# Layer 1 of six images by seven block products, and every set of seven products as seven tasks

## The chip, the core and the metric

The kernel runs on one core of a Trainium2 chip. The metric is device time in microseconds of one execution. The core has TensorE (PE, matrix products, with its weight loads listed apart as PEld), VectorE (DVE), ScalarE (ACT), GpSimd (POOL) and SyncE (SP), which mainly issues transfers (DMAs). Each engine works off its own instructions in order and waits on semaphores for the others. PE writes to PSUM[...]; everything else lies in SBUF.

## What is computed

Two layers run on x of shape (8, 32, 32, 256), all in float32. With N = 1024 tokens of C = 256 channels per image:

```
# layer 0, four heads of 256 channels
qkv   = xf @ W_qkv
atten = softmax over j of (q_i . k_j) / 16
res   = sum_j atten_ij v_j            # per head
x1    = concat(res) @ W_out + b_out + xf

# layer 1, 32 channels for f and g
f, g, h = x1 @ Wf + bf, x1 @ Wg + bg, x1 @ Wh + bh
b     = softmax over j of (g_i . f_j)
y     = gamma * (b @ h) + x1
```

The kernel folds the query and key weights of a head into one matrix, and the value and output weights into another, so that layer 0 needs only queries, scores, a product of the exponentials with x itself, and an output projection per head.

## The kernel before

**Units and steps.** A unit is one head of one image in layer 0 (`Layer0(b, h)`) or the whole layer 1 of one image (`Layer1(b)`). A unit has two blocks of 512 query tokens. A step is one block of one unit, and the list `steps` holds them in the order of the loop. Per image there are four layer-0 units, and layer 1 of the image before stands between head 1 and head 2 (`behind`), or behind head 3 for image 6 in the last round; layer 1 of image 7 is written out at the end.

**What a step issues.** The work is spread over three steps: step i issues the scores and half of the exponentials of its own block, the block sums, the key sums and most of the products of the block of step i-1, and the end of the products and the output projection of the block of step i-2. In the loop over `steps`, `put(tasks, *places)` gives each task a place, a number from about 0 to 10; at the end of the step the tasks are sorted by place and issued. PE, DVE and ACT keep exactly this order (`manual_schedule`); the planner orders POOL's and SP's instructions.

**Seven products.** `seven` (line 253 on, its matmuls on line 273) multiplies two matrices of 2 x 2 blocks with seven block products instead of eight, in three PSUM tiles z, y and x. `sum_a` and `sum_b` form the sums of blocks that it needs, four vector instructions each. It returns three tasks: `one` (products 1 and 6, copies e and u on ACT), `two` (products 5, 7 and 2, copy v, and the results 22 and 11), `three` (products 3 and 4, and the results 12 and 21). The results are vector additions of a PSUM tile and a copy (line 290). It serves the queries (`q`), the scores (`p`), the products of the exponentials with x (`y`) and the output projection (`o`).

**Layer 1 before.** `queries_apart` computes f and g (tile fg). `scores` makes 8 tiles of scores per block (`ps_l`, line 845) and their exponentials `s_l` (line 854). `values` computes h as rows for the image (`pr_v_l`, line 518, then line 828: times gamma, plus bias) with a column of ones behind it. `row_products` (line 933) multiplies the exponentials with these 257 columns, 8 matmuls for each of 4 tiles of tokens; the last column is the sum, and lines 941 and 943 divide and add x1.

**Sums and inverses of layer 0.** The block sums `ss` (line 638) are added up to `rs` (lines 645 and 649), `partition_all_reduce` on POOL (line 651) sums over the partitions into `rb`, two small transfers turn the row into columns (`line`, `st`), line 667 inverts, and two more spread the inverse over all partitions (`invb`). Line 725 scales the projection `o` by it, and a transfer issued on POOL (line 728) adds it to `x1T`. The sums `yt` of y (line 716) feed the output projection.

**Turning.** `squares` moves 32 x 32 squares by transfers, all issued on SP, and a vector transpose (line 418) turns each: from rows to columns for x (`turn_rows`), back for x1 (`turn_back`).

**Buffers.** The pools give the number of buffers per tag: `ps` 6 and `psm` 2 of the PSUM banks, `s` 2, `xT` 3, `v` 2, `m0` 1 (the tile o), `rs` 1, `rb` 1, `ss` 1.

Of the kernel before, what the change touches and what calls it, by code (L numbers as in the profile page):

```python
# [16 lines left out]
P = 128  # L17
# [3 lines left out]
def kernel(  # L21
# [67 lines left out]
    FAR = 2.0**64  # L89
# [163 lines left out]
    def seven(name, width, parts, matmuls, outs, tags, two_banks=False):  # L253
# [38 lines left out]
        def one():  # L292
            for k, number in (("z", 1), ("y", 6)):
                bank(k)
                product(k, number, k != "y" or not two_banks)
            nc.scalar.copy(scratch("e"), banks["z"])  # L296
            nc.scalar.copy(scratch("u"), banks["y"])

        def two():
            product("z", 5)  # L300
            product("y", 7)
            bank("x")
            product("x", 2, True)
            nc.scalar.copy(scratch("v"), banks["z"])  # L304
            add(outs["22"](), "y", sbs["v"])
            add(outs["11"](), "x", sbs["e"])

        def three():
            product("z", 3)
            product("y", 4)  # L310
            add(outs["12"](), "z", sbs["u"])
            add(outs["21"](), "y", sbs["e"])

        return [one, two, three]
# [64 lines left out]
    xT_of, x1T_of, xblocks, vblocks = {}, {}, {}, {}  # L379
# [16 lines left out]
    def squares(dst, src, swap):  # L396
# [5 lines left out]
        def move(a, c):  # L402
            for q in range(P // Q):
                to, rows_v = dst(), src()
                if swap:
                    nc.sync.dma_start(
                        to[ts(q, Q), :, c, ts(a, Q)], rows_v[ts(a, Q), c, :, ts(q, Q)]
                    )
                else:
                    nc.sync.dma_start(  # L410
                        to[ts(q, Q), c, :, ts(a, Q)], rows_v[ts(a, Q), :, c, ts(q, Q)]
                    )
# [48 lines left out]
    def value_sums(b):  # L461
# [3 lines left out]
        def piece(i):  # L465
            if i == 0:
                r = rows[b]
                t = tile_of("xt", [P, 4, NT // 2, P], f"xt_{b}")
# [3 lines left out]
                vblocks[b] = b_operands(blocks, sums)  # L472
# [61 lines left out]


    class Layer0:
# [82 lines left out]
        def sums(self, blk):  # L619
# [4 lines left out]
            made = {}  # L624

            def start():
                half = NT // 2
                p = self.p[blk]
                blocks = [p[:, ts(j, half), ts(e, HB)] for e in range(2) for j in range(2)]
                t = tile_of("ss", [P, 2, half, HB], f"ss_{n}")  # L630
                sums = [t[:, 1], t[:, 0], blocks[2], t[:, 0]]
                self.pblocks[blk] = a_operands(blocks, sums)
                made["t"], made["l"] = t, sum_a(sums, *blocks)

            def piece(i):
                if i == 0:
                    start()
                made["l"][i]()
# [8 lines left out]
            def last():  # L647
                r = made["r"]
                tt(r[:, 0, :], r[:, 0, :], r[:, 1, :], ALU.add)
                self.total[blk] = t = tile_of("rb", [P, NB], f"rb_{n}")  # L650
                nc.gpsimd.partition_all_reduce(  # L651
                    t, r.rearrange("p e i -> p (e i)"), P, bass_isa.ReduceOp.add
                )
                line = tile_of("line", [1, NB], f"line_{n}")
                nc.sync.dma_start(line, t[0:1, :])
                self.r[blk] = st = tile_of("st", [P, HT], f"st_{n}")
                with nc.allow_non_contiguous_dma(reason="a row of sums turns into columns"):
                    nc.sync.dma_start(st, line.rearrange("o (p t) -> p (o t)", p=P))

            adds = [partial(add, k) for k in range(1, NT // 2)]  # L660
            return [partial(piece, i) for i in range(4)], adds + [last]

        def invert(self, blk):
# [4 lines left out]
            if blk in self.rb:  # L668
                return
            line = tile_of("line", [1, NB], f"inv_{self.name}_{blk}")  # L670
            with nc.allow_non_contiguous_dma(reason="columns turn into a row"):
                nc.sync.dma_start(line.rearrange("o (p t) -> p (o t)", p=P), inv)
            self.rb[blk] = t = tile_of("invb", [P, NB], f"invb_{self.name}_{blk}")
            nc.sync.dma_start(t, line[0].partition_broadcast(P))
# [6 lines left out]
        def products(self, blk):  # L681


            def out(c, e):
                if blk not in self.y:
                    self.y[blk] = tile_of("y", [P, CC, NB], f"y_{self.name}_{blk}")
                return self.y[blk][:, c, ts(e, HB)].unsqueeze(1)

            return seven(
                f"y_{self.name}_{blk}", HB, 1,  # L690
                lambda number: [
                    (0, vblocks[self.b][number][:, j, :], self.pblocks[blk][number][:, j, :])
                    for j in range(NT // 2)
                ],
                {
                    "11": partial(out, 0, 0), "12": partial(out, 1, 0),
                    "21": partial(out, 0, 1), "22": partial(out, 1, 1),
                },
                NARROW,
            )  # L700

        def project(self, blk):
# [29 lines left out]
            return [partial(piece, i) for i in range(4)], seven(  # L732
# [7 lines left out]
            ), [add]  # L740


    class Layer1:
        scale = 1.0

        def __init__(self, b, direct=0):

            self.b, self.name, self.direct = b, f"{b}_l1", direct
            self.s = {}
            self.fg, self.v = None, None  # L750

# [23 lines left out]
        def queries_apart(self, tag=None):  # L775
# [7 lines left out]
            def task():  # L783
                fg = self.fg_tile()
                self.f, self.g = fg[:, 0, :], fg[:, 1, :]
                if tag is None:
# [33 lines left out]
        def values(self, last="psm"):  # L820
            def start():
                if self.v is None:
# [5 lines left out]
                lambda t2, pm: nc.vector.scalar_tensor_tensor(  # L828
                    self.v[:, 2 * t2 : 2 * t2 + 2, :C], pm, gamma_sb,
                    bh_sb.unsqueeze(1).broadcast_to([P, 2, C]), ALU.mult, ALU.add,  # L830
# [40 lines left out]
        def products(self, blk):  # L871
            return row_products(self, blk, rows1)

# [118 lines left out]
    steps, adds, exps = [], {}, {}  # L992

    for b in range(B):
        units = [Layer0(b, h) for h in range(HEADS)]
        if b > 0:
            units.insert(behind(b), Layer1(b - 1, NBLK))
        steps += [(u, blk) for u in units for blk in range(NBLK)]
# [9 lines left out]
    first_sums = value_sums(0)  # L1008
# [10 lines left out]
    for i, (a, blk) in enumerate(steps):  # L1019
        l0 = isinstance(a, Layer0)  # L1020
        one, two, nxt = step(i - 1), step(i - 2), step(i + 1)
        places = []

        def put(tasks, *at):
# [3 lines left out]
        if l0:  # L1028
            tasks, exps[i] = a.scores(blk)
            put(tasks, 0, 2, 4, 6, 8, 10)  # L1030
            put(exps[i][:2], 5.1, 6.1)
        else:
            tasks, _ = a.scores(blk)
            put(tasks, *((0.5, 2.4) if blk == 0 else (0.5, 2)))
        if is_l0(two):
            u, k = two
            put(u.products_of[k][2:], 1 if l0 else 0)
            if nxt is None:
                put([partial(u.invert_all, k)], 2.2)
            put([partial(u.invert, k)], 3.4 if l0 else 2.7)  # L1040
            ysums, tasks, adds[i] = u.project(k)
            put(ysums, *((1.1, 1.2, 1.3, 3.3) if l0 else (1.1, 1.2, 1.3, 2.5) if blk == 0 else
                         (0.6, 0.7, 0.8, 0.9)))
            put(tasks, *((3, 5.5, 7) if l0 else (4.5, 6, 7.2) if blk == 0 else
                         (3, 5, 7) if nxt else (1.9, 3.1, 4.1)))
            if nxt is None:
                put(adds[i], 4.2)
        if i - 1 in exps:
            put(exps[i - 1][2:], *((0.9, 0.91) if l0 else (0.1, 0.2)))
        if i - 1 in adds:  # L1050
            put(adds[i - 1], 0.5 if l0 or blk == 1 else 2.3)
        if is_l0(one):
            u, k = one
            sums, keys = u.sums(k)
            u.products_of[k] = u.products(k)
            put(sums, *((2.1, 3.2 if is_l0(two) else 2.4, 4.2, 5.6) if l0 else (0.8, 2.2, 3.5, 6.1)))
            put(keys, *((6.3, 6.6, 7.6, 8.7) if l0 else (6.3, 7.6, 8.3, 8.7)))
# [200 lines left out]
```

## Time and profile before

| | |
|---|---|
| median of 3 runs | 2305.96 us (2305.75 to 2306.03) |
| the profiled execution | 2305.9 us, of which its span is 2304.0 |
| PE busy | 2293.2 us, 10220 instructions |
| DVE busy | 1508.4 us, 2666 instructions |
| ACT busy | 756.9 us |
| POOL busy | 340.9 us |
| granted PE clock | 1.00 |
| layer-1 products, line 933 | 1024 PE instructions |
| layer-1 values, line 518 | 256 PE instructions |
| all-reduces, line 651 | 64, mean 3.226 us |
| transfers x1T<-o | 64, median 5.0 us from issue to landing |

Busy time is the time in which an engine has an instruction in work; the recorded durations of consecutive PE instructions overlap, so distances between starts are to be used for PE. A matmul in float32 appears as two PE records. In a line such as `psz<-q,xs 128x256 f32 x1024 | 264.6, 381` the names are the output and the inputs, then come shape and count, busy us and the mean ns of one. A bracket in the timeline tells how long the engine had been idle and what released it.

### The profile page before, as it was taken

How to read it: one execution, taken by the hardware profiler on the slowest of the kernel's cores; microseconds unless marked ns; L12 is line 12 of the kernel's file. 1: busy time of each engine (PE TensorE's matmuls, PEld its weight loads, DVE VectorE, ACT ScalarE, POOL GpSimd, SP SyncE). 2: the span in 40 equal slices, each digit the busy share in tenths (PEclk: the TensorE clock that was granted, in tenths of full speed). 3: DMA queues.
4: the chain of work that ended last, by engine and by line, in shares of the span. 5: the costliest groups of instructions: out<-in, count | busy, mean ns of one | idle time of the engine just before them, and what ended most of it. 6: DMA issues, size and time to landing. Idle time of an engine off the chain costs nothing.

```text
span 2304.0 us, 27262 instructions
## 1 busy us (share of the span) xinstructions
PE 2293.2 (100%) x10220; PEld 1887.2 (82%) x10220; DVE 1508.4 (65%) x2666; ACT 756.9 (33%) x1294; POOL 340.9 (15%) x243
## 2 busy tenths in 40 slices
PE   9999999999999999999999999999999999999999
PEld 7888888788887888788887888878888788888887
DVE  6776676476665766656766666656676557776663
ACT  3333333233332333323333233322333233333322
POOL 3111112011120112101121011210112101111211
PEclk9999999999999999999999999999999999999999
DMA  5111122301222113221132101321113211121222
GB/s 137 33 28 28 28 37 44 74 15 28 47 45 63 18 25 57 38 60 19 28 54 44 53 19 29 58 43 50 19 28 58 46 29 19 28 46 28 40 40 61
DMA packets 200925, 94.83 MB, mean 41 GB/s; under 512 B 165968, under 2 KB 170192, under 8 KB 200784
## 3 DMA queue, kind: packets, MB, share of 16 engines
q1 hardware_dynamic: 180176, 54.06, 11.2%
q0 software_dynamic: 20608, 38.94, 9.6%
q8 instruction: 83, 1.36, 0.2%
q14 instruction: 58, 0.48, 0.1%
HBM read 29.76 MB, written 8.65 MB: 17 GB/s over the span
## 4 chain that ended last, share of the span: by engine, by line
PE 98%; DVE 1%; DMA 1%; ACT 1%; issue 0%; ACTq 0%; SPq 0%
PE psz_y L273 14%; PE psy_y L273 14%; PE psz L273 14%; PE psy L273 14%; PE pa_l L933 10%; PE psz_o L273 7%; PE psx L273 5%; PE psx_y L273 5%; PE psz_q L273 3%; PE psy_q L273 3%; PE pr_v_l L518 3%; PE ps_l L845 1%; PE psx_q L273 1%; PE psx_o L273 1%; PE pm_fg L795 1%; DMA invb<-inv 0%
## 5 line engine op out<-in xcount | busy, mean ns | idle before, releaser
L651 POOL PARTITION_ALL_REDUCE rb<-rs x64 | 206.5, 3226 | 1448.8 <-issue 1153.4
L600 ACT ACTIVATE p<-p 128x1024 f32<-128x1024 f32 x256 | 263.9, 1056 | 74.5 <-DVE p L290 74.3
L273 PE MATMUL psz<-q,xs 128*128 128x256 f32 x1024 | 264.6, 381 | 0.0
L273 PE MATMUL psy<-qs,xs 128*128 128x256 f32 x1024 | 263.0, 379 | 1.2 <-DVE qs L579 1.2
L273 PE MATMUL psy_y<-p,xt 128*128 128x256 f32 x1024 | 241.9, 379 | 0.0
L933 PE MATMUL pa_l<-v_l,s_l 128*128 128x257 f32 x1024 | 232.1, 381 | 0.0
L273 PEld LDWEIGHTS psz<-q,xs 128*128 128x128 f32 x1024 | 192.9, 190 | 47.2 <-issue 19.1
L933 PEld LDWEIGHTS pa_l<-v_l,s_l 128*128 128x128 f32 x1024 | 193.7, 190 | 34.3 <-issue 6.8
L273 PEld LDWEIGHTS psy<-qs,xs 128*128 128x128 f32 x1024 | 193.3, 190 | 29.2 <-DVE qs L579 1.6
L296 ACT COPY e<-psz 128x512 f32<-128x512 f32 x128 | 75.1, 586 | 431.6 <-PE psz L273 431.6
L273 PEld LDWEIGHTS psy_y<-p,xt 128*128 128x128 f32 x1024 | 194.6, 190 | 26.4
L290 DVE TENSOR_TENSOR p<-psy,v 128x512 f32<-128x512 f32 x128 | 88.0, 688 | 87.7 <-ACT v L304 44.4
L728 POOL DMA_DIRECT2D x1T<-o x64 | 77.4, 1210 | 407.5 <-DVE o L725 354.2
L273 PE MATMUL psz<-q,x0T 128*128 128x256 f32 x512 | 131.4, 379 | 0.0
L273 PE MATMUL psx<-q,x0T 128*128 128x256 f32 x512 | 131.4, 379 | 0.0
L273 PE MATMUL psy<-qs,x0T 128*128 128x256 f32 x512 | 131.4, 379 | 0.0
L273 PE MATMUL psx_y<-p,x 128*128 128x256 f32 x512 | 121.0, 379 | 0.0
L273 PE MATMUL psz_y<-ss,x 128*128 128x256 f32 x512 | 121.0, 379 | 0.0
L273 PE MATMUL psy_y<-ss,xt 128*128 128x256 f32 x512 | 121.0, 379 | 0.0
L273 PE MATMUL psz_y<-p,x 128*128 128x256 f32 x512 | 120.9, 379 | 0.0
L273 PE MATMUL psz_y<-ss,xt 128*128 128x256 f32 x512 | 120.9, 379 | 0.0
L273 PEld LDWEIGHTS psz_y<-p,x 128*128 128x128 f32 x512 | 97.3, 190 | 20.9 <-PE psz_q L273 4.3
(153 smaller groups left out, 3700.5 us busy)
## 6 DMA issues: line engine op xcount, KB each, us to landing
x1T<-o POOLq DMA_DIRECT2D x64, 512.0 KB, 5.0
invb<-inv SPq DMA_DIRECT2D x63, 256.0 KB, 4.0
x<-x1T SPq DMA_DIRECT2D x256, 32.0 KB, 2.0
out_dram<-x SPq DMA_DIRECT2D x15, 512.0 KB
x<-in_x_dram SPq DMA_DIRECT2D x14, 512.0 KB, 4.4
x0T<-x SPq DMA_DIRECT2D x224, 32.0 KB, 2.0
fg<-v_l POOLq DMA_DIRECT2D x56, 64.0 KB, 2.0
w<-in_L_conv_W_qkv_dram POOLq DMA_DIRECT2D x36, 32.0 KB, 3.3
```

Source lines behind the costliest of these rows:

```text
L273: nc.tensor.matmul(banks[k][:, ts(i, w)], lhsT=lhsT, rhs=rhs, start=first and n == 0, stop=True, skip_group_check=True,)
L290: nc.vector.tensor_tensor(dst, shaped(banks[k]), shaped(other), ALU.add)
L296: nc.scalar.copy(scratch("e"), banks["z"])
L518: nc.tensor.matmul(pm[:, ts(j, C)], lhsT=src()[:, c, ts(2 * t2 + j, P)], rhs=w()[:, c, :], start=(c == 0), stop=(c == CC - 1),)
L600: exp(both, both)
L651: nc.gpsimd.partition_all_reduce(t, r.rearrange("p e i -> p (e i)"), P, bass_isa.ReduceOp.add)
L728: nc.gpsimd.dma_start(x1T_of[self.b][:, :, ts(blk, NB)], o, accum_op=ALU.add)
L795: nc.tensor.matmul(pm[ts(k, half)], lhsT=w[:, c, :], rhs=x1T_of[b][:, c, ts(k, NB)], start=(c == 0), stop=(c == CC - 1),)
L845: nc.tensor.matmul(pm, lhsT=self.f[ts(r, CK), ts(j0 + r, P)], rhs=self.g[ts(r, CK), ts(blk, NB)], start=True, stop=True,)
L933: nc.tensor.matmul(pm[:, : C + 1], lhsT=p[:, j, ts(ti, P)], rhs=v[:, j, : C + 1], start=(j == 0), stop=(j == NT - 1),)
```

## The change

**Layer 1 of images 0 to 5.** The product of the exponentials with the values is rearranged: instead of (exponentials) x (x1 Wh), it computes (exponentials x x1) first, by seven block products in the 2 x 2 scheme, and multiplies by Wh afterwards. The sums over keys no longer come from a column of ones. `weigh` adds up the eight tiles of exponentials with seven vector instructions, an all-reduce on POOL sums over partitions, and two small transfers turn the sums into columns. Since the columns of a block product share one set of inverses for both halves of a block, the exponentials of the second half of the 512 tokens are multiplied by the ratio of the halves' sums (`ratio`, `scale`). `block_sums` and `block_products`, which layer 0 now uses as well, do the rest, with sums of x1 rows (`value_sums`, now for either layer). `project` adds the bias to x1, multiplies by Wh and adds the result times the inverse. Wh is multiplied by gamma once. Layer 1 of images 6 and 7 keeps the old way.

**Order.** `seven` returns seven tasks instead of three, so that each product can have a place of its own. The layer-1 blocks of these six images no longer stand together: block 0, then block 0 of head 2, then block 1, then block 1 of head 2. For the steps of images 1 to 6 the table `PLACES` gives every task's place; the other images keep the old places.

**Transfers.** In `squares` every second transfer is now issued on POOL. `FAR`, a bound of the final check of inverses, changes from 2^64 to 2^60.

```diff
         def move(a, c):
             for q in range(P // Q):
                 to, rows_v = dst(), src()
+                queue = nc.sync if q % 2 else nc.gpsimd
...
-        return [one, two, three]
+        return [m1, m6, m5, m7, m2, m3, m4]
...
+    def sums_to_columns(r, n, order="o (p t) -> p (o t)"):
+        t = tile_of("rb", [P, NB], f"rb_{n}")
+        nc.gpsimd.partition_all_reduce(t, r, P, bass_isa.ReduceOp.add)
+        line = tile_of("line", [1, NB], f"line_{n}")
+        nc.sync.dma_start(line, t[0:1, :])
+        st = tile_of("st", [P, HT], f"st_{n}")
+        with nc.allow_non_contiguous_dma(reason="a row of sums turns into columns"):
+            nc.sync.dma_start(st, line.rearrange(order, p=P))
+        return t, st
...
+    def block_products(u, blk, of):
...
+        return seven(
+            f"y_{u.name}_{blk}", HB, 1,
+            lambda number: [
+                (0, of[u.b][number][:, j, :], u.pblocks[blk][number][:, j, :])
+                for j in range(NT // 2)
+            ],
...
+        def weigh(self, blk):
...
+            def add(k):
+                s = self.s[blk]
+                if k == 1:
+                    made["r"] = tile_of("rs", [P, NB], f"rs_{n}")
+                tt(made["r"], s[:, 0, :] if k == 1 else made["r"], s[:, k, :], ALU.add)
...
+            def ratio():
+                t = made["t"]
+                made["i"] = i = tile_of("rs", [P, HB], f"ratio_{n}")
+                nc.vector.reciprocal(i, t[:, HB:])
+                tt(i, i, t[:, :HB], ALU.mult)
+
+            def scale(k):
+                q = NT // 2
+                s = self.s[blk][:, ts(k, q), HB:]
+                tt(s, s, made["i"].unsqueeze(1).broadcast_to([P, q, HB]), ALU.mult)
...
+        def project(self, blk):
...
+                made["o"] = o = tile_of("m0", [P, HT, C], f"out_{self.name}_{blk}")
+                nc.vector.tensor_tensor(
+                    o, rows1[self.b][:, ts(blk, HT), :],
+                    bh_sb.unsqueeze(1).broadcast_to([P, HT, C]), ALU.add,
+                )
...
+            def task(t2):
+                pm = tile_of("psm", [P, NB], f"po_{self.name}_{blk}_{t2}")
+                y = self.y[blk]
+                for j in range(2):
+                    for c in range(CC):
+                        nc.tensor.matmul(
+                            pm[:, ts(j, C)],
+                            lhsT=y[:, c, ts(2 * t2 + j, P)],
+                            rhs=wh_sb[:, c, :],
+                            start=(c == 0),
+                            stop=(c == CC - 1),
+                        )
...
+    PLACES = {
...
+        "l0": {
+            "scores": (-0.286, 2.4),
...
+            "weigh": (6.324, 6.43, 7.407, 7.623, 7.822, 7.823, 8.536, 11),
...
+        "20": {
...
+            "scale": (-0.292,),
...
+            "sums of y": (0.599, 1.945, 2.149, 6.603),
+            "ratio": (2.411, 3.841, 4.1),
+            "own values": (0.786, 2.404, 2.551, 6.256),
...
-        if b > 0:
-            units.insert(behind(b), Layer1(b - 1, NBLK))
-        steps += [(u, blk) for u in units for blk in range(NBLK)]
+        order = [(u, blk) for u in units for blk in range(NBLK)]
+        if 0 < b < B - 1:
+            u = Layer1(b - 1, NBLK, True)
+            order[NBLK * behind(b) : NBLK * behind(b)] = [(u, 0)]
+            order[NBLK * behind(b) + 2 : NBLK * behind(b) + 2] = [(u, 1)]
+        elif b > 0:
+            u = Layer1(b - 1, NBLK)
+            order += [(u, blk) for blk in range(NBLK)]
+        steps += order
```

The keys of `PLACES` are head and block ("20" is head 2, block 0), "l0" and "l1" the layer-1 blocks.

## The prediction, made before the changed kernel had run

> **What bounds the kernel now.** I read the span and busy table of the page first, then the chain that ended last, then one whole image in stages, then single instructions in order of time.
>
> ```profile
> span 2304.0 us, 27262 instructions
> ...
> PE 2293.2 (100%) x10220; PEld 1887.2 (82%) x10220; DVE 1508.4 (65%) x2666; ACT 756.9 (33%) x1294; POOL 340.9 (15%) x243
> ...
> PE 98%; DVE 1%; DMA 1%; ACT 1%; issue 0%; ACTq 0%; SPq 0%
> ```
>
> TensorE (PE) is busy all the time and carries 98% of the chain. A matmul's recorded duration overlaps the next one's, so a busy PE need not be a full PE; the distance between starts decides. In the timeline, four instructions of 256 columns (two fp32 matmuls; each is two instructions) take 0.86 us from one row to the next:
>
> ```profile
> 1152.78 1.03 PE L273 MATMUL psz<-q,x0T 128*128 128x256 f32 x4
> ...
> 1153.64 1.03 PE L273 MATMUL psy<-qs,xs 128*128 128x256 f32 x4
> ```
>
> That is 0.215 us per instruction. The same holds for layer 1: 16 instructions of 257 columns run from 1000.82 to 1004.28 us, 0.216 us each. In the windows by image, images 1 to 6 each take 284 us, all alike:
>
> ```profile
> 870.50:1154.50 284.00, 283.85 (x1266) 233.47 (x1264) 185.00 (x325) 93.28 (x161) 39.59 (x25) 1.00 0.21 40
> ```
>
> The columns after the length are busy time and count of PE, weight loads, VectorE (DVE), ScalarE (ACT) and GpSimd (POOL), then the granted clock, 1.00. So each image is a full PE stream, and what changes the time is (a) how many PE instructions there are and (b) how long PE waits. The real waits are few. The largest comes once per image:
>
> ```profile
> 1154.35 0.42 DVE L290 TENSOR_TENSOR o<-psz_o,v_o 128x256 f32<-128x256 f32 x1 [2.77 <-ACT v_o L304]
> 1154.69 0.42 DVE L290 TENSOR_TENSOR o<-psx_o,e_o 128x256 f32<-128x256 f32 x1
> ...
> 1154.83 0.70 PE L273 MATMUL psz_o<-y,wo 128*128 128x256 f32 x2 [0.15 <-DVE o L290]
> ```
>
> PE starts 0.06 us after the vector result it needs is out. By the distances of starts this place costs 0.42 us (0.31 plus a slower second instruction). Nothing else in an image comes near it, apart from about 0.2 us at each switch to the small 32-row and 64-column matmuls, of which both kernels have the same number.
>
> [...] 381 ns recorded against 215 ns between starts. [...]
>
> ```profile
> 965.89 3.23 POOL L651 PARTITION_ALL_REDUCE rb<-rs  x1 [15.62 <-issue]
> ...
> 966.34 2.87 DVE L725 TENSOR_TENSOR o<-o,invb 128x1024 f32<-128x1024 f32 x1
> ```
>
> The scaling of o takes 1.215 us (its median over 64) and 2.87 beside an all-reduce. So an all-reduce holds a two-SBUF instruction off until about 0.45 + 1.65 = 2.1 us after its own start; instructions with a PSUM operand keep their 0.42 us beside it.[...]
>
> **The change, part by part.** Durations are those of the profiled run (2305.9 us: span 2304.0 and 1.9 around it; the median shown is 2305.96, the same).
>
> PE work. For six images, layer 1 now had 64 matmuls of 128x257 and 16 of 128x256 (values), 80 in all, 160 instructions. After: per block seven products of four matmuls (28), and 8 for the projection by Wh, so 72 matmuls, 144 instructions. 16 x 0.215 = 3.45 us less per image, 20.7 us in six. This part is nearly certain, since PE is the path.
>
> Waits of before. The place at psz_o above sits in steps whose order is all new for images 1 to 6: up to 6 x 0.42 = 2.5 us goes if nothing takes its place.
>
> DVE work. Issued back to back, vector instructions start 0.60 us apart for 512 columns (930.35, 930.95, 931.55 us), 0.34 for 256 (926.35, 926.70, 927.03) and about 1.15 for 1024. Per block added: seven sums of the exponentials 4.2, the ratio 0.8, two scalings 2.3, four block sums 4.6, four evacuations 1.4, bias 1.15. Per image twice that and four sums of x1 (2.4) make 31.3; removed are four value evacuations of 0.74 and eight reciprocals of 0.17, 4.3. So about 27 us more: 185 becomes 212 of 280. On average that hides. It is concentrated, though: in the three steps layer-1 block 0, layer-0 head 2 block 0, layer-1 block 1, PE has 68.2 us (counted from the instruction order at the prices above) and DVE issues about 64. There the vector queue has hardly any room.
>
> I walked that stage by hand, both queues in their new order, with zero at the start of the block-0 step. Two places come out late. First, the last query products of the step end at 21.5 on PE; the vector queue evacuates them to 22.3, then one sum, two o's and three query sums, whose third is out at 24.8. The first layer-0 product that reads it is due at 24.6: wait 0.25. Second, the sum for block 0's total ends at 28.75 and releases the all-reduce. The next vector instruction, the scaling of o (two SBUF inputs), starts at once and ends at 29.9; two PSUM evacuations follow to 30.7, and then the first sum of y, two SBUF inputs again.[...] Then the second sum of y is out at 35.1, and psz_o wants it at 33.9: wait 1.3. Without the lock it is out at 33.7: no wait. Bounds 0 and 1.3, and a little above if both lose; I take 0.8, since a time where DVE comes first was not to be seen in this trace. The remaining margins in the walk are thin (the second block sum before its product of head 3 block 1: 0.05 us; PSUM banks before the block-1 scores: about 1 us), so I add 0.3. Per image 0.25 + 0.8 + 0.3 = 1.35, six times 8.1 us. Bounds of this term: 0 and about 18.
>
> ACT: three copies of 128x256 more per block at 0.37, 1.1 us per block, in an engine busy 33%; hidden. The score and product copies stand in the same order behind their products.
>
> POOL and SP. POOL gets 12 all-reduces of 3.2 us (39 us) and half of the 256 + 224 turning transfers. At the 0.59 us per issue of the weight moves, which are of the same shape, 240 x 0.59 = 142 us. 341 + 181 is still under a quarter of the span. SP loses those 240. What they are moved past is the all-reduces and the accumulation of o on POOL, in order: all 16 of an image's return moves stand behind the last accumulation, which lands 5.0 us after issue, and before the next all-reduce. The steps are some 27 us, so that all-reduce isn't late. The transposes that read the turned tile come about a step later. I cost it at nothing; uncovered, a late turned tile stops the vector queue at the transpose, and PE shortly after.
>
> The new chain all-reduce, row to columns, ratio: the ratio stands 6 us behind the last sum in the vector queue, and the all-reduce is 3.2. In block 1 there are 5 us. Covered by about 2.
>
> m0 is one buffer, and the layer-1 output now takes it in turn with o. It must wait for o's accumulation (5.0 us) and is used about 7 us after o's scaling: covered by 1 to 2 us. Splitting the tasks and the added scaling of Wh (one 0.69 us instruction) cost nothing by themselves.
>
> Sum: 2305.9 - 20.7 - 2.5 + 8.1 = 2290.8, said as 2291.
>
> **The rivals.**
> 1. Clean: no new waits, 2305.9 - 20.7 - 2.5 = 2282.7. For it: DVE issues slightly less than PE in the tight stage, and most of what PE reads was out well ahead in the walk. Against: the two late places.
> 2. A transfer is late: turned tiles or m0 hold the vector queue about 1.5 us more per image: 2290.8 + 9 = 2299.8. For it: POOL now has 16 issues in a row, one buffer of m0. Against: a step's slack.
> 3. Slower: the vector queue takes the bound in the layer-1 stage. It issues 64 us in 68.2 and waits for PE in about five places of 1 us; once it is behind, each of three all-reduces adds its 1.65 in full. 4.95 + 0.25 = 5.2 per image, 31.2 against the 23.2 gained: 2314. It decides from 23.2/6 = 3.9 us per image. Against: the following step has PE 33.2 and DVE only about 21, so the lag cannot grow past one image.
> 4. The gain is all given back: within 0.2%, about 2301 to 2310; only if 1 and 3 meet half way.
>
> **How the numbers follow.** The forecast has 0.50, clean 0.23, the late transfer 0.14, slower 0.11, given back 0.02. A measurement of this kernel tells about 0.2% (4.6 us) from no change. Faster: 0.50 + 0.23 + 0.11 of the third case = 0.84; same: 0.03 of the third and 0.02 = 0.05; slower 0.11. The range leaves out the slower case, the upper third of the late-transfer case and a margin below clean: 2282 to 2300.
>
> **What would show it.** PE records fall from 10220 to 10124. The rows psz_y, psy_y, psx_y of layer 1 hold 0.215 us between starts. In the windows an image takes about 281.5 us; under 281 means clean, over 284 slower. The first psz_o after the layer-1 block-0 step waits for the sum of y[...]. If PE waits for a DMA or a transpose, the second rival is right. A DVE that is busy through the stage with PE waiting at most places is the third. If PE's instructions take more than 0.215 us in the new products, the first term itself is wrong.

## The result and the profile after

The changed kernel takes 2299.3 us (median of 8 runs, 2298.5 to 2299.6), the kernel before 2305.8 (8 runs). The ratio is 0.9972 (95% interval 0.9961 to 0.9982). So it is faster, but by 6.5 us where 14.9 were forecast: 2291 was said, and 2299.3 lies at the upper end of the range.

The page of the kernel after, the busy table and the chain:

```profile
span 2297.4 us, 27586 instructions
...
PE 2277.7 (99%) x10124; PEld 1869.5 (81%) x10124; DVE 1706.9 (74%) x2871; ACT 774.7 (34%) x1330; POOL 522.5 (23%) x489
...
PE 98%; DVE 1%; issue 0%; DMA 0%; ACT 0%; DVEq 0%
```

PE lost exactly the 96 instructions forecast, and still carries 98% of the chain. It fell from 100% to 99% busy: the new thing is idle time. In the windows by image (length, then busy time and count of each engine), one image of the kernel after:

```profile
675.70:958.40 282.70, 280.92 (x1250) 230.53 (x1248) 215.92 (x359) 95.68 (x167) 65.25 (x58) 1.00 0.21 40
```

An image takes 282.7 us, where it took 284.0 and where 281.5 were forecast. Without any new wait it would be 284.0 - 3.45 - 0.42 = 280.1. So 2.6 us of waits came in per image; the forecast had 1.35. They all lie in two neighbouring steps: layer 1's first block ("l0") and head 2's first block ("20").

The first one, in the timeline of the kernel after (start, duration, what; the bracket is the engine's idle time before and who ended it):

```profile
958.16 0.59 PE L273 MATMUL psx_o<-y,wvo 128*128 128x256 f32 x2
...
958.36 0.37 ACT L317 COPY v_o<-psz_o 128x256 f32<-128x256 f32 x1 [5.28 <-PE psz_o L273]
958.77 0.42 DVE L290 TENSOR_TENSOR o<-psz_o,v_o 128x256 f32<-128x256 f32 x1
...
959.25 0.70 PE L273 MATMUL psz_o<-y,wo 128*128 128x256 f32 x2 [0.49 <-DVE o L290]
```

This is the place of the kernel before over again, at another spot: product 3 of o comes right behind product 2, and has to wait until product 5's result has gone through ACT and DVE. By starts, 1.09 us pass where two instructions take 0.43: by the unrounded times this costs 0.65 us, and 0.10 more in the instruction behind it.

The largest one comes 10 us later:

```profile
964.94 1.22 DVE L758 TENSOR_TENSOR o<-o,invb 128x1024 f32<-128x1024 f32 x1
...
965.18 4.07 POOL L556 PARTITION_ALL_REDUCE rb_l<-rs_l  x1 [9.83 <-DVE rs_l L927]
...
966.86 1.68 DVE L749 TENSOR_TENSOR yt<-y 128x256 f32<-128x256 f32 x1
...
969.40 0.68 DVE L290 TENSOR_TENSOR p<-psy,v 128x512 f32<-128x512 f32 x1
970.00 0.67 DVE L290 TENSOR_TENSOR p<-psx,e 128x512 f32<-128x512 f32 x1
...
970.13 0.70 PE L273 MATMUL psy<-qs,x0T 128*128 128x256 f32 x2 [1.12 <-DVE p L290]
```

Beside the all-reduce (4.07 us here, where the scaling of o began 0.24 us before it; 3.23 in most other places of this trace) the first sum of y takes 1.68 instead of 0.42 us, as the forecast had it; this delay, as measured, is called the lock below. The two evacuations ahead of it (966.08 and 966.41) keep their 0.42 and 0.41. But PE doesn't wait for that sum. It waits for an evacuation (p<-psy,v) that stands three instructions behind it on DVE: product 4 adds onto psy and must not before psy's old content is read. By starts: 1.29 us and 0.10 behind it.

The third is product 6 of layer 1 (psy_y_l), 0.22 and 0.07 us in the image shown and up to 0.33 in others, behind a group that the forecast had priced at 0.8 us together. In the groups by line (count, then busy us and mean ns of one):

```profile
L937 DVE RECIPROCAL ratio_l<-rb_l 128x256 f32<-128x256 f32 x12 | 20.9, 1740 | 0.0
L938 DVE TENSOR_TENSOR ratio_l<-ratio_l,rb_l 128x256 f32<-128x256 f32 x12 | 5.1, 425 | 0.4
```

The three sum to 2.4 us; some 0.2 of the 2.6 are spread over places too small to be named. One sentence in the description of the change is not right: images 0 and 7 don't keep the old places; their layer-0 steps take the table's entries "00" and "01".

### The profile page after: what moved, and what is told of

The parts are those of the page before. It is cut to its first block, busy times and chain, and to the rows that moved or that the text cites. A ratio compares the mean times of both kernels' runs of the same rounds, so it can differ in the third digit from the quotient of the medians.

```text
span 2297.4 us, 27586 instructions
## 1 busy us (share of the span) xinstructions
PE 2277.7 (99%) x10124; PEld 1869.5 (81%) x10124; DVE 1706.9 (74%) x2871; ACT 774.7 (34%) x1330; POOL 522.5 (23%) x489
## 4 chain that ended last, share of the span: by engine, by line
PE 98%; DVE 1%; issue 0%; DMA 0%; ACT 0%; DVEq 0%
PE psz_y L273 14%; PE psy_y L273 14%; PE psy L273 14%; PE psz L273 14%; PE psz_o L273 7%; PE psx_y L273 5%; PE psx L273 5%; PE psz_q L273 4%; PE psy_q L273 4%; PE psy_y_l L273 3%; PE psz_y_l L273 3%; PE pa_l L1051 2%; PE po_l L973 2%; PE ps_l L887 2%; PE psx_q L273 1%; PE psx_o L273 1%
## 5 line engine op out<-in xcount | busy, mean ns | idle before, releaser
L273 PE MATMUL psy_y<-p,xts 128*128 128x256 f32 x1024 | 241.9, 379 | 0.0
L273 PEld LDWEIGHTS psy_y<-p,xts 128*128 128x128 f32 x1024 | 194.6, 190 | 26.5
L308 ACT COPY v<-psz 128x512 f32<-128x512 f32 x128 | 74.8, 585 | 159.3 <-PE psz L273 159.3
L273 PE MATMUL psy_y<-ss,xts 128*128 128x256 f32 x512 | 121.6, 380 | 0.0
L273 PE MATMUL psz_y<-ss,xts 128*128 128x256 f32 x512 | 121.0, 379 | 0.0
L273 PEld LDWEIGHTS psy<-qs,x0T 128*128 128x128 f32 x512 | 96.8, 190 | 22.1 <-DVE p L290 9.1
```

The source lines that it names most:

```text
L273: nc.tensor.matmul(banks[k][:, ts(i, w)], lhsT=lhsT, rhs=rhs, start=first and n == 0, stop=True, skip_group_check=True,)
```

## The experiments

Two theories stood at the start. **T1, one backlog:** from 955.8 us on the vector queue in these steps is never idle for 25 us; it is the local bound, and the waits of PE are where it shows. **T2, separate waits:** each has its own cause and goes alone. All kernels below start from the changed one (2299.3 us) unless said; ratios are to the kernel before, with 95% intervals.

**1. No all-reduce.**

```diff
-    def sums_to_columns(r, n, order="o (p t) -> p (o t)"):
+    def sums_to_columns(r, n, order="o (p t) -> p (o t)", reduce=True):
...
-        nc.gpsimd.partition_all_reduce(t, r, P, bass_isa.ReduceOp.add)
+        if reduce:
+            nc.gpsimd.partition_all_reduce(t, r, P, bass_isa.ReduceOp.add)
+        else:
+            nc.gpsimd.memset(t, 1.0)
...
-                    made["r"], n, "o (t p) -> p (o t)"
+                    made["r"], n, "o (t p) -> p (o t)", False
```

> The changed kernel with the all-reduce over the partitions of the new layer-1 blocks (two in each of six images) replaced by a memset on the same engine; the sum over the partitions is left out, everything else stands in its place. The changed kernel takes 2299.3 us. Theory T1 (the vector queue is the local bound in the step of layer 1's first block and the one behind it, and the waits of the TensorE there are one backlog): beside no all-reduce, yt<-y is back from 1.68 to 0.42 us, the wait before product 4 of the first score group of step 20 (1.29 + 0.10 us an image) is gone, and what the vector queue saves also shortens later ones: 8 to 10 us in all, 2289 to 2291 us. Theory T2 (separate waits, each with its own cause): that wait alone goes, 8.3 us, 2291 us, and the waits before psz_o (0.65) and psy_y_l1 (0.22 to 0.33) stay as they are. Rival (the all-reduce has nothing to do with it, the order of the vector queue alone makes the wait): no change, 2299 us.

Measured: 2291.8 us, ratio 0.9938 (0.9924 to 0.9951). Its timeline, the same instructions of the same image:

```profile
964.64 0.42 DVE L752 TENSOR_TENSOR yt<-y 128x256 f32<-128x256 f32 x1
...
965.92 0.68 DVE L290 TENSOR_TENSOR p<-psy,v 128x512 f32<-128x512 f32 x1
```

The sum of y is back at 0.42 us and the evacuation follows 1.28 us behind it instead of 2.54. The wait for psy is gone; the other two stay to the hundredth (0.65, 0.22). 7.5 us in six images are 1.25 each, the very length of the stall. So without the lock the largest wait isn't there. T1's surplus did not come, which alone would favour T2. But it doesn't yet show that the lock alone is the cause: the wait would also go if 1.3 us of any other work left the vector queue ahead of that evacuation. Later runs test that.

**2. No reciprocal.**

```diff
-                nc.vector.reciprocal(i, t[:, HB:])
-                tt(i, i, t[:, :HB], ALU.mult)
+                tt(i, t[:, HB:], t[:, :HB], ALU.is_equal)
```

> The changed kernel with the reciprocal and the multiplication of the ratio in the new layer-1 blocks replaced by one comparison of the same size; the ratio is left out. It takes 1.75 us of the vector queue away in each of twelve blocks. If the reciprocal's length is what the sixth product of layer 1 waits for (psy_y_l1, 0.22 to 0.33 + 0.07 us): this wait goes and no other, 2 to 2.5 us in all, 2297 us. If the whole backlog of the two steps hung on the length of the vector queue (the strong form of T1), the score groups around it would gain too, 4 to 6 us, 2294 us. If the reciprocal is hidden: no change, 2299 us.

Measured: 2297.6 us, ratio 0.9963 (0.9949 to 0.9976). The wait of psy_y_l is gone and nothing else has moved: 1.75 us in all, 0.29 per image, a little under the 2 to 2.5 expected; the 4 to 6 us of T1's strong form did not come. DVE work that comes at the end of the stretch is worth only the wait that follows it, not its length.

**3. Two additions of the row sums later.**

```diff
-            "weigh": (6.324, 6.43, 7.407, 7.623, 7.822, 7.823, 8.536, 11),
+            "weigh": (7.36, 7.37, 7.407, 7.623, 7.822, 7.823, 8.536, 11),
```

> The changed kernel with the first two additions of the row sums in the step of layer 1's first block (place l0) put behind the third query sum, 6.32 and 6.43 to 7.36 and 7.37; same work. T1 (one backlog of the vector queue): the wait before product 3 of psz_o (0.65 + 0.10 us an image) goes, but the all-reduce starts no earlier and the wait before product 4 of the first score group of step 20 is as long or longer: no gain, 2298 to 2301 us. T2 (separate waits): the wait before psz_o goes alone, 4.5 us, 2295 us.

Measured: 2311.0 us, ratio 1.0022 (1.0013 to 1.003), 11.7 us more than the changed kernel. A miss for both theories in size, and the most telling run. The wait before psz_o stayed at 0.65 us although the additions were gone from in front of it: it is the chain ACT, DVE, PE itself, whatever the queue holds. The timeline of DVE shows it idle there until ACT has copied v_o:

```profile
962.85 0.42 DVE L290 TENSOR_TENSOR o<-psz_o,v_o 128x256 f32<-128x256 f32 x1 [0.58 <-ACT v_o L317]
```

In place of the two additions DVE idled for 0.43, 0.17 and 0.58 us, and never got that back. From the last evacuation of y to that of psy DVE needs 15.1 us instead of 13.6, and PE waits 2.74 us for it instead of 1.29. The timeline of PE:

```profile
972.07 1.03 PE L273 MATMUL psz<-q,xs 128*128 128x256 f32 x4
975.67 1.49 PE L273 MATMUL psy<-qs,x0T 128*128 128x256 f32 x4 [2.58 <-DVE p L290]
976.96 1.06 PE L273 MATMUL psz_o<-y,wvo 128*128 128x256 f32 x2
977.81 1.06 PE L273 MATMUL psz_o<-yt,wo 128*128 128x256 f32 x2
```

And behind the wait two instructions of PE lie 0.85 us apart instead of 0.43. The window there gives the granted clock, third number from the end, as 0.66 on average:

```profile
976.00:981.00 5.00, 5.00 (x17) 3.91 (x16) 4.91 (x8) 1.23 (x3) 0.00 (x0) 0.66 0.68 105
```

This came in three of the six images. 0.66 over 5.00 us is half the clock for about 3.4 us (an estimate: 5.00 x 0.34 / 0.5), and seven or eight instructions lose about 1.5 us together (0.43 instead of 0.215 us each). In the other three the same wait of 2.74 us cost nothing more. In the profiled execution, 12.9 us longer than that of the changed kernel, the longer waits make 8.7 (six times 1.45) and the slow stretches 4.6; 0.9 go off, since psy_y_l doesn't wait in the three images with a slow stretch, and some 0.5 stay unnamed.

**4. Sums of y behind the evacuation.**

```diff
-            "sums of y": (0.599, 1.945, 2.149, 6.603),
+            "sums of y": (1.994, 1.996, 2.149, 6.603),
-            "own values": (0.786, 2.404, 2.551, 6.256),
+            "own values": (1.995, 2.404, 2.551, 6.256),
```

> The changed kernel with the first two sums of y and the first sum of the own values of step 20 put behind the evacuation of the first score group (places 0.60, 1.95 and 0.79 to 1.99); same work, so that no instruction of the vector engine with two inputs in SBUF stands between the scaling of o and the evacuation that the TensorE waits for. If the lock at the all-reduce is the cause of the wait before product 4 of that group (1.29 + 0.10 us an image): it goes, 8 us in all, 2291 us, and the stall beside the all-reduce falls on instructions that nobody waits for. If the vector queue is the bound of the stretch as a whole (T1), part of it comes back at the next evacuations: 3 to 6 us, 2294 to 2296 us.

Measured: 2296.6 us, ratio 0.996 (0.9946 to 0.9973), 2.7 us less, a little below T1's 3 to 6. The timeline of DVE:

```profile
964.99 0.41 DVE L290 TENSOR_TENSOR y<-psy_y,e_y 128x256 f32<-128x256 f32 x1
965.97 0.69 DVE L290 TENSOR_TENSOR p<-psy,v 128x512 f32<-128x512 f32 x1 [0.56 <-PE psy L273]
966.76 0.69 DVE L290 TENSOR_TENSOR p<-psx,e 128x512 f32<-128x512 f32 x1
967.37 0.41 DVE L749 TENSOR_TENSOR yt<-y 128x256 f32<-128x256 f32 x1
```

The wait of PE for psy is gone and the sum of y takes 0.41 us, clear of the lock. But the stall of 1.26 became idle time of 0.56 and about 0.2 behind it, in front of instructions that now come later; PE waits for the sum of y at psz_o (0.52 and 0.10) and longer at psy_y_l (0.59 instead of 0.22). 1.26 - 0.76 = 0.5 per image; measured 0.45. That is T1: what counts is the time of the vector queue, not which instruction is held up.

**5. Three products of o ahead of those of y.**

```diff
-            "project": (2.681, 6.667, 7.455),
+            "project": (2.681, 6.29, 7.455),
```

> The changed kernel with products 5, 7 and 2 of o in step l0 put ahead of products 5, 7 and 2 of y (place 6.667 to 6.29), so that 7.3 us of other products of the TensorE lie between product 2 of o and product 3 of o; same work. In the changed kernel the TensorE waits there for a chain: product 5 ends, ScalarE copies v_o (0.37), VectorE adds (0.42). Chain theory: the wait before product 3 of psz_o (0.65 + 0.10 us an image) goes, and the two additions of o leave the full stretch of the vector queue, so the wait before psy, product 4, gets no longer: 4 to 5 us in all, 2294.5 to 2295 us. Backlog theory (the PE merely reaches the next wait sooner, because the VectorE is the bound from there on): the wait before psy grows by what was saved, 2298 to 2299 us; as the two additions (0.68 us) have gone to an earlier place, at least some gain should stay.

Measured: 2302.3 us, ratio 0.9985 (0.9979 to 0.9992): 3.0 us slower than the changed kernel, which neither theory expected. Its timelines of DVE and of PE:

```profile
956.27 0.42 DVE L290 TENSOR_TENSOR y<-psy_y,v_y 128x256 f32<-128x256 f32 x1 [1.53 <-PE psy_y L273]
957.93 0.42 DVE L290 TENSOR_TENSOR y<-psx_y,e_y 128x256 f32<-128x256 f32 x1 [1.23 <-PE psx_y L273]
```

```profile
960.31 1.03 PE L273 MATMUL psz<-q,x0T 128*128 128x256 f32 x4
962.34 0.89 PE L273 MATMUL psy<-qs,xs 128*128 128x256 f32 x3 [1.00 <-DVE qs L657]
```

The chain theory held for its own wait: psz_o follows the query product without a gap. But PE then reached the query sums too soon and waited 1.16 us for them, and later still 1.38 for psy. The account of DVE explains the loss: the moved products delay the last evacuation of y by 1.29 us in PE's order, and from there to the evacuation of psy DVE takes 12.9 us instead of 13.6. 1.29 - 0.73 = 0.56 per image later; measured 0.51. Removing a wait of PE cost time: what DVE saved behind its last evacuation of y (0.73) is less than what that evacuation lost by the new order (1.29), and PE then waited for DVE elsewhere.

**6. Five additions of the row sums early.** If DVE is the bound from 955.8 us on, work must go to where it idles before (0.79, 0.91 and 1.23 us). The tile rs has one buffer, taken there by layer 0's own row sum, so the sum of the first block lies in a free quarter of x1s.

```diff
-                    made["r"] = tile_of("rs", [P, NB], f"rs_{n}")
+                    made["r"] = (
+                        tile_of("rs", [P, NB], f"rs_{n}") if blk
+                        else self.x[:, 3].rearrange("p t c -> p (t c)")
+                    )
...
-            "weigh": (6.324, 6.43, 7.407, 7.623, 7.822, 7.823, 8.536, 11),
+            "weigh": (2.43, 3.83, 3.84, 6.31, 6.312, 7.36, 7.37, 11),
```

> The changed kernel with five of the seven additions of the row sums of layer 1's first block moved from the full stretch of the vector queue (places 6.32 to 8.54) to where it is idle (2.43, 3.83, 3.84, 6.31, 6.31) and two to 7.36 and 7.37; for this the sum of the first block lies in a free quarter of another tile (x1s); same work. Backlog theory (the vector queue of this stretch is the bound, 24.1 us of work from the last eviction of y to the sum that product 6 of layer 1 waits for, against 22.0 us of the TensorE): about 2 to 3 us of vector work leave the stretch, the all-reduce starts 1 to 2 us earlier, its stall falls on an instruction that nobody waits for soon, and the waits before psy (1.39) and psy_y_l1 (0.3) go: 8 to 10 us in all, 2289 to 2291 us. Lock theory (only the meeting with the all-reduce matters): where the stall meets another sum that the TensorE needs, the wait moves there, and the gain is under 3 us, 2296 to 2299 us.

Measured: 2289.4 us, ratio 0.9931 (0.9917 to 0.9944): 9.9 us below the changed kernel, in T1's range. Its timeline of POOL and DVE, the two all-reduces, the two instructions that met them, and what follows up to the evacuation of psy:

```profile
949.78 3.23 POOL L556 PARTITION_ALL_REDUCE rb<-rs  x1 [14.05 <-issue]
950.79 2.49 DVE L930 TENSOR_TENSOR x1s<-x1s,s_l 128x512 f32<-128x512 f32 x2
...
958.71 3.23 POOL L556 PARTITION_ALL_REDUCE rb_l<-x1s  x1 [5.69 <-DVE x1s L930]
959.13 2.10 DVE L657 TENSOR_TENSOR qs<-q,qs 128x256 f32<-128x256 f32 x1
961.15 1.21 DVE L758 TENSOR_TENSOR o<-o,invb 128x1024 f32<-128x1024 f32 x1
...
964.34 0.68 DVE L290 TENSOR_TENSOR p<-psy,v 128x512 f32<-128x512 f32 x1
```

The lock lasts 2.1 us from the start of each all-reduce; it even costs twice, 2.49 for a pair that takes 1.41 and 2.10 for a sum that takes 0.42. But at 959 us DVE is ahead, PE doesn't need the sum yet, and no wait for psy is left (psy_y_l 0.11 and 0.07). So the lock is enough to cause this wait only where the queue is already full: from the last evacuation of y to that of psy DVE takes 13.6 us in the changed kernel, 12.4 without the all-reduce (first run) and 10.8 here, and at 12.4 only 0.1 us of wait is left. What stays is the chain of psz_o. In the windows, an image takes 281.0 us:

```profile
904.00:1185.00 281.00, 280.51 (x1250) 230.55 (x1248) 217.06 (x359) 95.51 (x167) 64.62 (x58) 1.00 0.22 41
```

The 280.1 without new waits and the 0.75 + 0.18 left give 281.0.

**7. Five and six together.**

> Both moves together: products of o earlier and additions of the row sums earlier. If the three waits have the causes named, all of them go (2.5 to 2.7 us an image): 2283 to 2286 us, the forecast's clean case. If the TensorE meets a new wait as soon as it runs ahead, 2288 to 2292 us.

Measured: 2289.9 us, ratio 0.9932 (0.9919 to 0.9946), no better than the sixth alone. The psz_o wait (0.75) went and one at the query sums came (0.56 and 0.07), and psy_y_l rose to 0.19 and 0.07: the second of the two expected cases.

**8. What is left of the change without its block products.** Here `weigh`, `block_sums` and `block_products` are not used for layer 1; its blocks stand together again, and the layer-0 steps of every image take the places "00" and "01".

```diff
-        if 0 < b < B - 1:
+        if b > 0:
-            u = Layer1(b - 1, NBLK, True)
-            order[NBLK * behind(b) : NBLK * behind(b)] = [(u, 0)]
-            order[NBLK * behind(b) + 2 : NBLK * behind(b) + 2] = [(u, 1)]
+            u = Layer1(b - 1, NBLK)
+            order[NBLK * behind(b) : NBLK * behind(b)] = [(u, blk) for blk in range(NBLK)]
...
-        mid = new or (l0 and 0 < a.b < B - 1)
+        mid = False
```

> The changed kernel with layer 1 of all images computed as in the kernel before (values of layer 1 by rows, no block products, no ratio, no sums of blocks), and with the seven tasks, the splitting of the transfers over two queues and the places of images 0 and 7 for every image: what is left of the change without its block products. If these parts cost nothing, as the forecast has it: the time of before, 2303 to 2308 us. If the seven tasks or the transfers by themselves carry a cost or a gain: outside of that. The places are not made for the steps beside layer 1, so a slower time would leave open which of the parts it is; one not slower clears all three.

Measured: 2303.0 us, ratio 0.9989 (0.9983 to 0.9996), 2.6 us less than before. That is the term "waits of before" of the forecast (up to 2.5). The place of psz_o that cost the kernel before 0.42 us an image, in its timeline:

```profile
1152.53 1.03 PE L273 MATMUL psy<-qs,xs 128*128 128x256 f32 x4
1153.39 0.59 PE L273 MATMUL psz_o<-y,wo 128*128 128x256 f32 x2
1153.82 0.59 PE L273 MATMUL psz_o<-yt,wvo 128*128 128x256 f32 x2
```

0.86 and 0.43 us between starts: no wait. As that wait accounts for the whole difference, seven tasks, split transfers and these places together cost nothing here, which the forecast had as an estimate. With this, the block products, with the order and the places made for them, took the kernel from 2303.0 to 2299.3: 20.7 us of matmuls less, and some 17 us of waits more.

**9 and 10. The chain of psz_o filled.** From the kernel of the sixth run. The three products of y between product 2 and product 3 of o are five microseconds of work; in the tenth, one sum of x1s also goes behind.

```diff
-            "product": (2.986, 3.254, 6.296, 6.306, 6.316),
+            "product": (2.986, 3.254, 6.68, 6.69, 6.7),
-            "weigh": (2.43, 3.83, 3.84, 6.31, 6.312, 7.36, 7.37, 11),
+            "weigh": (2.43, 3.83, 3.84, 6.668, 6.669, 7.36, 7.37, 11),
-            "first queries": (6.749, 7.171, 7.349, 7.952),
+            "first queries": (6.66, 6.661, 6.662, 7.952),
```

> The kernel with the early additions of the row sums (2289.4 us), and with products 5, 7 and 2 of y in step l0 moved between product 2 and product 3 of o (places 6.296, 6.306, 6.316 to 6.68, 6.69, 6.70), two of the early additions behind them, and the first three query sums to 6.66; same work. There a wait of 0.65 + 0.10 us an image before product 3 of psz_o is left. If it is the chain of product 5, copy of v_o and addition on the VectorE, then 5.2 us of other products cover it, and the last two query products end 6.5 us ahead of the query sums' use instead of 3.8: the wait goes and no other takes its place, 4.5 us, 2285 us. If the vector queue is still the bound of the stretch, its end does not move: 2289 us; if the additions of y, which now end later, hold up the query sums or the scaling of o, slower than 2289 us.

The tenth adds:

```diff
-            made["l"][i]()
+            made["l"][(1, 2, 0, 3)[i] if callable(tag) else i]()
...
-            "own values": (0.786, 2.404, 2.551, 6.256),
+            "own values": (2.404, 2.551, 5.6, 6.256),
```

> The same kernel with the first of the own values' sums (x1s, needed only by product 7 of layer 1) moved from 0.79 to 5.6 in step 20; same work. It takes 0.60 us of the vector queue from ahead of the sum that product 6 of layer 1 waits for (0.11 + 0.07 us an image left). If that wait is the last of the backlog: about 1 us less than the kernel beside it, 2284 us; if the queue there has caught up by now: no change.

Measured: 2304.3 us, ratio 0.9992 (0.9984 to 1.0), and 2322.4, ratio 1.0075 (1.0061 to 1.0089). Both missed by far. In the ninth the three known waits are gone, as expected, and a larger one has come, from a dependence that I had not looked up. Its timeline:

```profile
956.85 0.66 DVE L290 TENSOR_TENSOR q<-psy_q,v_q 128x512 f32<-128x512 f32 x1
...
957.56 1.13 PE L273 MATMUL psy_q<-x0T,wt 128*128 128x512 f32 x2 [2.46 <-DVE q L290]
```

Product 4 of the queries adds onto psy_q, which DVE reads at 956.85, behind 2.6 us of row sums. With the products of y gone from in front of it, PE came there 5 us earlier. The tenth has that wait and one of 1.93 us at product 7 of layer 1: place 5.6 in the sum's queue is behind four long block sums, not in front of its use. And behind the wait of psy_q instructions of PE run at half rate again, in the ninth in two of the six images (at 389.71 us two take 0.86 us by starts instead of 0.43), in the tenth in all six; the mean granted clock of the whole execution is 0.998 and 0.995, in the changed kernel 1.00.

**11. The queries' evacuations ahead of the row sums.** From the ninth.

```diff
-            "queries": (0.946, 1.784, 3.52, 5.701, 6.131, 6.345, 6.355),
+            "queries": (0.946, 1.784, 3.52, 4.05, 4.06, 6.345, 6.355),
```

> The kernel with the chain of o filled (2304.3 us) with products 7 and 2 of the next queries at 4.05 and 4.06 in step l0 in place of 5.70 and 6.13, so that the two evictions that product 4 of the queries waits for stand ahead of the row sums of layer 0 on the VectorE; the order of the TensorE and the work are the same. In the kernel beside it the TensorE waits 2.62 us there, in every one of six images, and in two of those looked at its matmuls run at half speed for some microseconds behind that. If the cause is the place of the evictions on the vector queue: this wait goes, no matmul runs slower, and as the waits of the changed kernel (psz_o 0.75, psy 1.39, psy_y_l1 0.3) were gone already, the time is that of the forecast's clean case, 2283 to 2286 us. If the row sums of layer 0, later by 1.2 us, or their all-reduce hold up the query sums in turn: 2288 to 2295 us.

Measured: 2289.1 us, ratio 0.9927 (0.9913 to 0.994): 15.3 us less than the ninth, and the same as the sixth, not the 283 to 286 of the clean case. The 2.62 us are gone; 0.33 at psy and 0.29 at psy_y_l are back. The timeline of DVE says why:

```profile
951.79 1.50 DVE L657 TENSOR_TENSOR qs<-q 128x256 f32<-128x256 f32 x1
...
958.78 2.10 DVE L657 TENSOR_TENSOR qs<-q,qs 128x256 f32<-128x256 f32 x1
```

Two sums of 0.42 us met an all-reduce each (at 950.78 and 958.35 us, 3.23 us long), 1.1 and 1.7 us lost, in a queue that has no idle time over 0.2 us from 940 to 975 us. DVE is the bound again.

The sixth and the eleventh kernel, both the full computation, are the fastest: 2289.4 and 2289.1 us against 2299.3 of the change and 2305.8 before. Between the two no difference can be told. Not tried: taking the reciprocal, or one of the all-reduces, off this stretch while keeping the result.

## Why the prediction was right and wrong

**PE work, 20.7 us: right.** 96 records less, and the new products keep their 0.43 us from pair to pair.

**Waits of before, up to 2.5 us: right in size.** The eighth run, without the block products, shows 2.6. The term held "if nothing takes its place", though, and a wait of the same chain did, at another spot (0.75 an image, below).

**New waits, 1.35 per image, 8.1 us: this step failed.** By images it was 2.6; by the medians it was 2299.3 - (2305.8 - 20.7 - 2.6) = 16.8 us in all, near the upper bound of 18. That the bound still held is in part luck, as more than a quarter of it, the chain of psz_o, came from a place that the sum doesn't contain. Taken apart:

- *The lock, priced at 0.8 between 0 and 1.3.* The meeting and its length were right: the scaling of o ended at 966.16, and the sum of y was held off until about 968.1 (966.86 + 1.68 - 0.42), 2.0 us later, where the walk took the 2.1 measured beside an all-reduce of the kernel before. What holds it off was not shown; that it goes with the all-reduce, the first run shows. The upper bound was the value to take: with the lock 1.39, without it 0.1 (first run). The victim was wrong. I followed the held-up instruction to its own reader, psz_o; PE stood before an evacuation queued behind it. And it is a wait only because the queue ahead of it was full (sixth run).
- *The second query sum's 0.25* did not come. A wait of that kind showed only where PE was brought there earlier (fifth and seventh run).
- *Thin margins, 0.3.* This sum had to hold two things that my walk had missed. The psz_o chain, 0.75 an image: I had named the place in the kernel before and taken it for gone, without asking where its seven tasks stand in the new order. And the reciprocal: the ratio was priced at 0.8 us for both instructions and took 2.1. The reciprocal alone took 1.74 us, against 0.42 for an addition of the same shape. It was worth 0.29 an image.

The price of the reciprocal was to be had. The page gives none, but the trace of the kernel before does, in its groups by line:

```profile
L679 DVE RECIPROCAL invb<-rb 128x512 f32<-128x512 f32 x1 | 3.3, 3344 | 0.0
```

An estimate from this line, for half the columns half of 3.34 us, is about 1.7 us, which is what was measured.

**The rivals.** Clean (2282.7) was not reached by any kernel here, though its terms are right. The late transfer was not seen: no PE wait in the two steps is ended by a transfer. The third, the vector queue as the bound of this stage, was right in mechanism and put at 0.11: experiments 3, 4, 5, 6 and 11 all move as DVE's account says. It didn't cost the 5.2 us per image that I gave it: in the image shown, three vector instructions are held off beside an all-reduce, by 1.26, 0.78 and 1.67 us (at 966.9, 1013.7 and 1130.0), and PE waits only behind the first. The walk had said that DVE issues 64 us in 68 and has "hardly any room", and then priced single late places as if the rest of the queue were free. T2 was right on one point: the psz_o chain doesn't depend on the queue.

**What would show it.** The image of 281.5 was forecast and is 282.7, between "as forecast" and "slower". Of the signs, the wait of psz_o for the sum of y was not there, though that sum took 1.68 us beside the all-reduce. The sign of the third rival was there by half: DVE is busy through the stage, with no idle time shown from 956 us on, but PE waits at three places and not at most.

## What to carry to other kernels

Where two engines' work in a stretch is nearly equal, keep the account of the second one: from its last idle time to the instruction that the first one needs, add up what it issues and what it is held off, and compare the stretches; a wait taken from the first engine then may cost time (3.0 us in the fifth run), and work moved to where the second one idles may pay (9.9 us in the sixth). An instruction that is held up delays what is queued behind it (the evacuation of psy came 2.54 instead of 1.28 us behind the start of the sum of y), so look for the reader of those too. And before moving a product, look up what its accumulator has to have been read by.

## What the runs showed of the hardware that was not expected

A wait of PE had a price beyond its length. Behind waits of 2.6 to 2.7 us by starts (idle times of 2.46 to 2.58 us in the brackets) PE ran at half rate for about 3.4 us, the estimate from the window of the third run (0.66 granted over 5.00 us), in three of six images of that run, two of the ninth and all six of the tenth; up to eight instructions were then 0.43 instead of 0.22 us apart. Behind 1.29 us it does not show (the changed kernel, 1.00 in the window of the image), nor behind 1.93 us (the tenth run, where the eight instructions from 995.15 us on take 1.81 us). What decides between the images of one run was not tested.

The lock was shorter than the all-reduce. In the sixth run the two held-off instructions can go on 2.1 us after the start of an all-reduce of 3.23 us (950.79 + 2.49 - 1.41 - 949.78, and 959.13 + 2.10 - 0.42 - 958.71), as in the kernel before (965.89, and 966.34 + 2.87 - 1.215). And the all-reduce itself takes longer at times: in the changed kernel 4.07 us in the six places where the scaling of o began 0.24 us before it, and the other all-reduces of this size take 3.2 to 3.5.
